# Quarter-wise stores, early loads for the second batch, and two moved pieces of setup in a fused graph network kernel

## The chip, the cores and the metric

The kernel runs on one core of one Trainium2 chip. The metric is the device time of the whole program in microseconds. A core has TensorE (PE) for matrix products, VectorE (DVE), ScalarE (ACT) and GpSimd (POOL) for the rest, and SyncE (SP), which here only issues transfers. POOL issues transfers too. The engines run side by side, each in its own program order, and wait for one another through semaphores.

## The reference

The input `x` has 128 samples of 128 nodes with 256 channels, `adj` is 128 x 128 for each sample, everything in float32. Two layers, each with a normalization in front and a residual:

```python
h = jnp.maximum(_layernorm(x, axis=-1), 0.0)
x = x + _L0_gnn_ref(h, adj, ...)
h = jnp.maximum(_layernorm(x, axis=-1), 0.0)
x = x + _L1_gnn_ref(h, adj, W1, b1, W2, b2, fusion_w)
```

Layer 0 computes from `h` a pointwise convolution, a convolution with 17 taps along the nodes with a residual, and a message passing term (a three-channel embedding, `exp` of minus squared distances, a product with `relu(x w_msg + b)`); both go into the gates of a GRU, 256 wide. Layer 1 takes five groups of the first 25 nodes (53 rows together), runs two graph convolutions on each (256 to 512 to 256), and adds the results, weighted with a softmax of the five `fusion_w`. So layer 1 changes only rows 0 to 24 of a sample; the other rows of the result are layer 0's.

## The kernel before

**Tiling.** Four samples make one `q`; there are 32 of them. The 17-tap convolution is done in a transformed domain of 80 points along the nodes, in two batches of 16 q each. Layer 1 works on blocks of four q (16 samples), eight blocks.

**Stages.** For each batch there is a *begin* and then *products*. The begin (`stage_a`, one call for each q) loads x of the q (`load_x`, L360, four transfers of 128 KB on SP's queue), takes mean and variance with `bn_stats` and `bn_aggr` on DVE and a `pow` on POOL (`moments`, L267 to L270), normalizes on DVE (L275), transposes on PE (`ph`, L387), stores the result to memory as `hTd` through POOL (L392), multiplies with the first convolution's weights (`pc`, L398) and transforms (`pf`, L409) into the large tile X. The products (`stage_b`) run over 40 frequencies f: load weights `wf` on SP (L488, three frequencies ahead), add on POOL (`add`, for f + 1), multiply on PE (`pa`, `pb`, L502), combine on DVE into `y` (L525), and store `yd` through POOL. Beside the first begin runs `tap_weights`, which transforms the convolution's weights (`pw`, L451) and stores them as `wfd`; beside everything after it runs `early(q)`, the message passing of each q (`pse`, `pm`, `pd`, `px`). Then a last, long stage runs the inverse transform and the gates for each q (`stage_c`), with what is left of `early`, and layer 1 (`rows`, `prepare`, `block`) beside it.

**What sets the order.** The order of the instructions is written by the program itself, when it is built. Every helper is a generator that yields two numbers: the time it believes its PE work takes, and the time until it can go on. `Lane` holds a row of such generators, of which `ahead` run at once; `Order.run` always takes the lane that has done least for its weight, and in it the one that is due. The second begin runs three lanes: `begin` with three q at a time, `beside` with weight 0.2, and `gates` (`fold_gates`, which loads and combines the gates' weights) with weight 0.5. What is late in a yield only fixes the place of an instruction in its engine's queue; on the chip the engine waits for what the instruction needs.

**Names that matter here.** In `stage_a`, a q loads itself and its successor, and if its own x was not there before, it yields 6 us (or 14 for the later ones of the second batch) before its statistics. `load_late` (L252, L253) loads `wse` (67 KB) and the second part of the constants `cst` (461.5 KB) on SP; it is called from `tap_weights` at step (n, m) = (2, 4) of 4 x 8. Nothing needs them before the end of that stage, in `fold_embedding`. The pool `tw`, closed when `tap_weights` ends, holds `wse`, two `wt`, one `wide` and three `ws` tiles of 16 KB per partition, and the pools `wg`, `io` and `fr` are opened in the same memory right after; a tile there waits until what lay in its place has been read or stored. `wmsg` and `bmsg` (L474, L475) are the first loads into `fr`, and the first loads of `hT` (L540) into `io` follow them on SP.

**The end.** `block` runs the two graph convolutions of a block and then, for each of its four quarters (one q each): `turn` (transposes on PE, L1062, a copy on ACT), `gather` (PE, L1074; then an addition on DVE, L1076, and a relu on ACT, L1077), `fuse` (PE with the fusion weights `s2w`, L1083; then an addition into x1 on DVE, L1085). Then four transfers on POOL's queue (L1094) store x1 of all four quarters. `setup_1` prepares layer 1; it loads `fus` and makes the softmax of the fusion weights on DVE and ACT (L895 to L906) into `s2w`.

Of the kernel before, what the change touches and what calls it, by code (L numbers as in the profile page):

```python
# [19 lines left out]
P = 128  # L20
# [187 lines left out]
def kernel(ctx: ExitStack, tc: tile.TileContext, x, adj, consts, vecs, w_se, conv1_w,  # L208
# [24 lines left out]
    def c(name):  # L233
        a, b = CAT[name]
        return cst[:, a:b]
# [13 lines left out]

    def load_late():  # L250

        nc.sync.dma_start(out=wse, in_=w_se.rearrange("(k p) o -> p k o", p=P))  # L252
        nc.sync.dma_start(out=cst[:, CFIRST:], in_=consts[:, CFIRST:])  # L253

    scl, sft = {}, {}
    brz = cp.tile([P, 4], FP, name="brz")
    wse9 = wp.tile([P, 2, WIDE], FP, name="wse9")
# [70 lines left out]
    def fold_embedding():  # L328
# [9 lines left out]
                                       op0=ALU.mult, op1=ALU.add)  # L338
        yield 1.5, 0.0

    lab, turn = ExitStack(), []
# [24 lines left out]
    def stage_a(q):  # L368
        ab = LATE["ab"]
        for n in range(q, min(q + 2, (q // BQ + 1) * BQ)):  # L370
            if n not in XA:
                load_xa(n)
                if n == q:
                    yield 0.0, 14.0 if q > BQ else 6.0
        if q not in MOM:
            MOM[q] = moments(XA[q], "a")
            yield 0.0, 3.0
            normalize(XA[q], XA[q], *MOM[q])
            yield 0.0, 2.0
        while q - 2 >= q // BQ * BQ and q - 2 not in A_DONE:  # L380
            yield 0.0, 0.5
        xn = XA[q]
        hT = ab.tile([P, 2, 512], FP, tag="hTa", name=f"hTa{q}")
        for cc in range(2):
            ph = ptmp.tile([P, 4, GB, WIDE], FP, tag="tmp", name=f"ph{q}_{cc}")
            for t in range(4):
                nc.tensor.transpose(ph[:, t].rearrange("p j n -> p (j n)"),  # L387
                                    xn[:, t, cc * P:(cc + 1) * P], ident)
            nc.scalar.activation(
                hT[:, cc].rearrange("p (j t n) -> p t j n", j=GB, t=4), ph, AF.Relu)  # L390
        yield 0.9, 2.4
        nc.gpsimd.dma_start(out=hTd[q], in_=hT)  # L392
        h1 = ab.tile([P, GB, D], FP, tag="h1", name=f"h1{q}")
        for h in range(2):
            pc = ptmp.tile([P, 2, D], FP, tag="tmp", name=f"pc{q}_{h}")
            for i in range(2):
                for k in range(2):
                    nc.tensor.matmul(pc[:, i], hT[:, k, (2 * h + i) * N:(2 * h + i + 1) * N],  # L398
                                     c1w[:, k], start=(k == 0), stop=(k == 1))
            s = slice(2 * h, 2 * h + 2)  # L400
            nc.vector.tensor_tensor(h1[:, s], pc, brow[:, None, :].to_broadcast([P, 2, D]),
                                    ALU.add)
            nc.scalar.activation(h1[:, s], h1[:, s], AF.Relu)
            yield 1.75, 2.8 * h
        for h in range(2):
            for k in range(2):
                pf = ptmp.tile([P, 2, D], FP, tag="tmp", name=f"pf{q}_{k}_{h}")
                for i in range(2):
                    nc.tensor.matmul(pf[:, i, :F * NB], h1[:, 2 * h + i, k * P:(k + 1) * P],  # L409
                                     fwd, start=True, stop=True)  # L410
                g0 = (q % BQ * GB + 2 * h) * NB
                dst = X[:, k, :, g0:g0 + 2 * NB].rearrange("p f (g b) -> p f g b", b=NB)
                src = pf[:, :, :F * NB].rearrange("p g (f b) -> p f g b", b=NB)
                if (k, h) == (0, 0):
                    nc.vector.tensor_copy(dst, src)  # L415
                else:
                    nc.scalar.activation(dst, src, AF.Copy)
            yield 1.1, 0.0
        A_DONE.add(q)
# [16 lines left out]
    def tap_weights():  # L436

        yield 0.0, 16.0
        for n in range(4):
            for m in range(8):  # L440
                if m == (0 if n else 3) and n < 3:
                    load_taps(n + 1, nc.sync, nc.gpsimd)
                if (n, m) == (2, 4):
                    load_late()
                if m % 2 == 0:
                    ws = tw.tile([P, 4, 4, D], FP, tag="ws", name=f"ws{n}_{m}", bufs=3)
                pws = [(pgat if r < 3 else ptmp).tile([P, 2, D], FP, tag="gat" if r < 3 else "tmp",
                                                      name=f"pw{n}_{m}_{r}") for r in range(4)]
                for r in range(4):
                    rows = slice(32 * r, 32 * r + TAPS)  # L450
                    nc.tensor.matmul(pws[r][:F], c("tap")[rows], wts[n][rows, 2 * m:2 * m + 2],  # L451
                                     start=True, stop=True)
                i = m % 2 * 2
                for r in range(4):
                    if r < 2 or (r == 2 and m % 2):
                        nc.scalar.activation(ws[:F, r, i:i + 2], pws[r][:F], AF.Copy)
                    else:
                        nc.vector.tensor_copy(ws[:F, r, i:i + 2], pws[r][:F])
                yield 0.9, 2.2
                if m % 2:  # L460
                    for r in range(4):
                        i0 = 64 * r + 16 * n + 2 * (m - 1)
                        nc.gpsimd.dma_start(out=wfd[:, i0:i0 + 4], in_=ws[:F, r])
# [4 lines left out]
        LATE["wn"] = wg.tile([P, 7, 2, P], FP, name="wn")  # L468
        LATE["wh"] = wg.tile([P, 7, 1, P], FP, name="wh")
        LATE["io"] = near.enter_context(tc.tile_pool(name="io", bufs=2, reuse_waits="tile"))  # L470
        LATE["fr"] = near.enter_context(tc.tile_pool(name="fr", bufs=1, reuse_waits="tile"))
        LATE["wmsg"] = LATE["fr"].tile([P, 2, D], FP, name="wmsg")
        LATE["bmsg"] = LATE["fr"].tile([P, D], FP, name="bmsg")
# [4 lines left out]
    def stage_b(bat):  # L478
# [29 lines left out]
        for f in range(NF + 1):  # L508
            if f + 3 <= NF:
                load_w(f + 3)  # L510
            if f < NF:
                add(f + 1)
            y = xf.tile([P, 2, D], FP, tag="y", name=f"y{bat}_{f}")
            pa = pgat.tile([P, 2, D], FP, tag="gat", name=f"pa{bat}_{f}")
            for s in range(2):
# [355 lines left out]
    def setup_1():  # L871
# [6 lines left out]
            tc.tile_pool(name="l2", bufs=2, reuse_waits="tile"))  # L878
        b2s = pool.tile([NG, D], FP, tag="dd", name="b2s")
        nc.sync.dma_start(out=b2s, in_=b2)  # L880
        fus = pool.tile([P, NG], FP, name="fus")
        nc.sync.dma_start(out=fus, in_=fusion_w.partition_broadcast(P))
        for n in range(2):
            load_w1(n)
        S["w2"] = weight(pool, W2, [P, 5, 4, D], "g (k p) o -> p g k o", "w2", nc.sync)
# [4 lines left out]
        for t in (*r4, S["yz"][:, 0], S["yz"][:, 1], S["b1"]):  # L890
            nc.gpsimd.memset(t, 0.0)
            yield 0.0, 4.0

        fmx = pool.tile([P, 1], FP, name="fmx")
        nc.vector.reduce_max(fmx, fus, axis=mybir.AxisListType.X)  # L895
        nc.vector.tensor_scalar(fus, fus, fmx, None, op0=ALU.subtract)  # L896
        nc.scalar.activation(fus, fus, AF.Exp)
        fsm = pool.tile([P, 1], FP, name="fsm")
        nc.vector.reduce_sum(fsm, fus, axis=mybir.AxisListType.X)
        nc.vector.reciprocal(fsm, fsm)  # L900
        nc.vector.tensor_scalar(fus, fus, fsm, None, op0=ALU.mult)
        nc.vector.tensor_mul(fus, fus, c("grp"))
        wrow = pool.tile([P, 1], FP, name="wrow")
        nc.vector.reduce_sum(wrow, fus, axis=mybir.AxisListType.X)
        s2w = S["s2w"] = pool.tile([P, 2 * WIDE], FP, name="s2w")
        nc.vector.tensor_scalar(s2w, c("s2"), wrow, None, op0=ALU.mult)  # L906
        b2row = S["b2row"] = pool.tile([P, D], FP, name="b2row")
        pb2 = ptmp.tile([P, 512], FP, tag="tmp", name="pb2")
        nc.tensor.matmul(pb2[:, :D], c("grpt")[:NG], b2s, start=True, stop=True)
# [92 lines left out]
    def block(blk):  # L1002
        while not (blk in P_DONE and blk - 1 in B1_DONE):
            yield 0.0, 0.5
        pool, yz, b2row, s2w = S["pool"], S["yz"], S["b2row"], S["s2w"]
        w2, ac, r4 = S["w2"], S["ac"][blk % 2], S["r4"][blk % 2]

        for q in range(QS):
# [48 lines left out]
        def turn(q):  # L1057
            pz = ptmp.tile([P, 2, D], FP, tag="tmp", name=f"pzt{blk}_{q}")
            for a in range(2):
                for cc in range(2):  # L1060
# [1 line left out]
                    nc.tensor.transpose(  # L1062
                        pz[:, a, cc * P:(cc + 1) * P],
                        yz[:, cc, b0:b0 + 2, :].rearrange("p s r -> p (s r)"), ident)
            zt = zts[q] = pool.tile([P, 2, D], FP, tag="zt", name=f"zt{blk}_{q}", bufs=3)
            nc.scalar.activation(zt, pz, AF.Copy)

        def gather(q):
# [10 lines left out]
        def fuse(q):  # L1079
            zt = zts.pop(q)  # L1080
            pf = ptmp.tile([P, D], FP, tag="tmp", name=f"pfu{blk}_{q}")
            for a in range(2):
                nc.tensor.matmul(pf[a * 2 * WIDE:(a + 1) * 2 * WIDE], s2w, zt[:, a],  # L1083
                                 start=True, stop=True)
            nc.vector.tensor_add(x1[:, q], x1[:, q], pf)  # L1085

        for what, q in ((turn, 0), (turn, 1), (turn, 2), (gather, 0), (gather, 1), (fuse, 0),
                        (turn, 3), (gather, 2), (fuse, 1), (gather, 3), (fuse, 2), (fuse, 3)):
            what(q)
            if (what, q) == (gather, QS - 1):  # L1090
                B1_DONE.add(blk)
            yield {turn: 0.45, gather: 0.9, fuse: 0.5}[what], 0.5
        for j in range(GB):
            nc.gpsimd.dma_start(  # L1094
                out=out[blk * SB:(blk + 1) * SB, :WIDE].rearrange("(q j) n c -> j n q c", j=GB)[j],
                in_=x1[j * WIDE:(j + 1) * WIDE])
        F_DONE.add(blk)


# [5 lines left out]
    load_xa(2)  # L1105
    fold()
    beside = Lane([tap_weights()] + [early(q) for q in range(NQ)])
    gates = Lane([fold_gates()], weight=0.5)
    for bat, (during_a, during_b) in enumerate(((0.66, 0.5), (0.2, 0.65))):
        if bat:  # L1110
            take_turn("ab", 2, reuse_waits="tile")
# [58 lines left out]
```

## Time and profile before

| | us |
|---|---|
| median of three runs | 2099.61 |
| lowest and highest of the three | 2089.95, 2099.69 |
| the profiled execution: device time | 2107.02 |
| its span, first to last instruction | 2105.2 |
| last matmul ends | 2098.1 |
| mean granted clock of TensorE in it | 0.986 |

The table by stage and the waits that matter are shown in the prediction. In such a table each row is a stretch of the span; for every engine it gives the time it was busy and, in brackets, how many instructions it ran. The granted clock is the share of full speed at which TensorE was allowed to run. In a list of waits each row reads: engine, tile, line, then what it waited for, the total in us, how often, and the longest. In a line of the timeline the first number is the start, the second the time, and the text in square brackets says how long the engine was idle before and what released it. "SPq" is SyncE's queue, where "x4" are four transfers issued in a row, and the second number is the time from the first to the end of the last issue.

The first 222 us are the first begin, 222 to 371 the first products, 371 to 540 the second begin, 540 to about 708 the second products; then comes the long last stage. From 2062 us on, only block 7 of layer 1 is left.

### The profile page before, as it was taken

What the parts mean: (1) busy time and instruction counts of PE and PEld (TensorE: products, weight loads), DVE (VectorE), ACT (ScalarE), POOL (GpSimd) and SP (SyncE); (2) the same over time, 40 slices, a digit from 0 to 9 for tenths busy, and PEclk for the clock granted to TensorE, in tenths of its full rate; (3) what the DMA queues carried; (4) which work ended last, traced back from release to release, by engine and by line L of the source; (5) the groups of instructions that cost most, each with busy time, mean ns of one, the idle gap of its engine ahead of it and who ended that gap; (6) DMA issues with size and microseconds to landing.
All of it is one profiled execution on the core that took longest, in us unless ns stands there. A gap on an engine that the chain in (4) does not pass through costs nothing.

```text
span 2105.2 us, 31050 instructions
## 1 busy us (share of the span) xinstructions
PE 2045.2 (97%) x11316; PEld 1657.3 (79%) x11316; DVE 1181.8 (56%) x2775; ACT 686.8 (33%) x1543; POOL 725.5 (34%) x902
## 2 busy tenths in 40 slices
PE   7978999999999999999999999999999999999998
PEld 5656888789888788787878877878787787878875
DVE  6754544786544455655654565565565655654642
ACT  4643222344222333323232232232233223223333
POOL 3432666232565222503322233224323323233230
PEclk9989999999999999999999999999999999999999
DMA  9977778744777634222323332323232333223121
GB/s 217 276 227 231 240 266 264 211 153 143 250 258 257 210 111 141 75 78 73 89 71 92 87 83 72 88 71 91 75 96 73 79 91 93 78 81 98 31 79 51
DMA packets 186870, 281.67 MB, mean 134 GB/s; under 512 B 20745, under 2 KB 139982, under 8 KB 186718
## 3 DMA queue, kind: packets, MB, share of 16 engines
q1 hardware_dynamic: 156270, 185.00, 31.0%
q0 software_dynamic: 30160, 94.46, 14.1%
q8 instruction: 90, 1.47, 0.3%
q14 instruction: 62, 0.51, 0.1%
q10 hardware_dynamic: 288, 0.22, 0.0%
HBM read 187.34 MB, written 92.27 MB: 133 GB/s over the span
## 4 chain that ended last, share of the span: by engine, by line
PE 91%; DMA 4%; DVE 2%; issue 1%; POOL 1%; ACT 0%; SPq 0%; POOLq 0%; DVEq 0%; ACTq 0%
PE p L709 41%; PE pa L502 7%; PE pm L601 5%; PE ph L1031 5%; PE pz L1040 5%; PE pc L398 4%; PE pb L502 3%; PE pi L674 3%; PE px L627 3%; PE pf L409 2%; PE pg L1074 1%; PE ph L387 1%; PE pc L688 1%; PE po L855 1%; DMA xa<-in_x 1%; PE py L1014 1%
## 5 line engine op out<-in xcount | busy, mean ns | idle before, releaser
L835 POOL TENSOR_TENSOR d<-hTc,r 128x512 f32<-128x512 f32 x64 | 81.3, 1271 | 370.9 <-ACT r L832 370.9
L502 PE MATMUL pa<-wf,X 128*128 128x256 f32 x640 | 152.5, 381 | 0.0
L864 POOL DMA_DIRECT2D out<-xt x128 | 71.9, 567 | 211.0 <-DVE xt L861 205.4
L525 DVE SCALAR_TENSOR_TENSOR y<-pa,kk 128x512 f32<-128x512 f32 x78 | 53.8, 690 | 147.0 <-ACT kk L524 147.0
L398 PE MATMUL pc<-c1w,hTa 128*128 128x256 f32 x512 | 125.4, 392 | 6.6 <-DVE X L415 4.3
L709 PE MATMUL p<-th,wrz 128*128 128x256 f32 x512 | 131.7, 380 | 0.0
L724 ACT ACTIVATE z<-z,brz 128x256 f32<-128x256 f32 x128 | 58.1, 501 | 225.5 <-DVE z L781 191.2
L709 PE MATMUL p<-tc,wrz 128*128 128x256 f32 x512 | 131.6, 380 | 0.0
L709 PE MATMUL p<-tm,wrz 128*128 128x256 f32 x512 | 131.5, 380 | 0.0
L502 PEld LDWEIGHTS pa<-wf,X 128*128 128x128 f32 x640 | 118.3, 190 | 16.2 <-issue 2.2
L601 PE MATMUL pm<-wmsg,hT 128*128 128x256 f32 x512 | 124.4, 389 | 0.0
L691 DVE SCALAR_TENSOR_TENSOR xc<-pc,s_bn,hTc 128x256 f32<-128x256 f32 x128 | 53.1, 478 | 118.3 <-PE pc L688 118.3
L398 PEld LDWEIGHTS pc<-c1w,hTa 128*128 128x128 f32 x512 | 96.0, 195 | 25.9 <-DVE X L415 4.5
L601 PEld LDWEIGHTS pm<-wmsg,hT 128*128 128x128 f32 x512 | 97.9, 194 | 16.7 <-issue 1.8
L1031 PE MATMUL ph<-yz,w 128*128 128x96 f32 (+3 forms) x640 | 109.2, 325 | 0.9 <-DVE yz L1016 0.9
L1033 ACT ACTIVATE hh<-ph,vec 128x96 f32<-128x96 f32 (+3 forms) x160 | 64.0, 402 | 134.2 <-PE ph L1031 124.7
L709 PEld LDWEIGHTS p<-tm,wrz 128*128 128x128 f32 x512 | 97.5, 190 | 13.0
L1040 PE MATMUL pz<-hh,w 128*128 128x96 f32 (+3 forms) x640 | 107.3, 322 | 0.0
L1031 PEld LDWEIGHTS ph<-yz,w 128*128 128x128 f32 x640 | 88.1, 193 | 21.9 <-issue 13.2
L709 PEld LDWEIGHTS p<-tc,wrz 128*128 128x128 f32 x512 | 95.2, 190 | 12.0 <-issue 0.5
L709 PEld LDWEIGHTS p<-th,wrz 128*128 128x128 f32 x512 | 94.9, 190 | 12.1 <-DVE fus L896 0.3
L709 PE MATMUL p<-hTc,wrz 128*128 128x256 f32 x384 | 103.9, 394 | 0.0
(204 smaller groups left out, 4562.0 us busy)
## 6 DMA issues: line engine op xcount, KB each, us to landing
wf<-wfd SPq DMA_DIRECT2D x160, 256.0 KB, 4.1
wfd<-ws POOLq DMA_DIRECT2D x64, 320.0 KB, 8.2
yd<-y POOLq DMA_DIRECT2D x80, 256.0 KB, 3.8
yt<-yd SPq DMA_DIRECT2D x64, 320.0 KB, 4.9
w<-in_W SPq DMA_DIRECT2D x40, 512.0 KB, 3.7
xa<-in_x SPq DMA_DIRECT2D x128, 128.0 KB, 5.2
hTd<-hTa POOLq DMA_DIRECT2D x32, 512.0 KB, 5.8
hT<-hTd SPq DMA_DIRECT2D x32, 512.0 KB
```

The costliest lines, as they stand in the source:

```text
L398: nc.tensor.matmul(pc[:, i], hT[:, k, (2 * h + i) * N:(2 * h + i + 1) * N], c1w[:, k], start=(k == 0), stop=(k == 1))
L502: nc.tensor.matmul(ps, xk(k), WF[f][:, k, s], start=(k == 0), stop=(k == 1))
L601: nc.tensor.matmul(pm[:, i], hT[:, k, j * N:(j + 1) * N], LATE["wmsg"][:, k], start=(k == 0), stop=(k == 1))
L627: nc.tensor.matmul(px[:, dc, i], msgs[h][:, i, dc * P:(dc + 1) * P], aT[:, 2 * h + i], start=True, stop=True)
L674: nc.tensor.matmul(pi[b * 64:(b + 1) * 64], inv[:F], yt[:, b::2], start=True, stop=True)
L709: nc.tensor.matmul(ps[:, m], w[:, i, k, m * P:(m + 1) * P], factor(i, x, t), start=first and j == 0, stop=last and j == len(n) - 1, skip_g ...
L724: nc.scalar.activation(dst[:, m], src[:, m], AF.Sigmoid, bias=brz[:, b + m:b + m + 1])
L835: nc.gpsimd.tensor_sub(d, hT[:, dc], r[:, dc])
L864: nc.gpsimd.dma_start(out=out[q * GB + j, WIDE:].rearrange("(t n) c -> n t c", n=WIDE), in_=xt[j * WIDE:(j + 1) * WIDE, 1:4])
L1031: nc.tensor.matmul(ph, w1[:, k, m * P:(m + 1) * P], yz[:, k, :, o:o + n], start=(k == 0), stop=(k == 1))
L1033: nc.scalar.activation(hh[:, m], ph, AF.Relu, bias=v("b1", g * 4 + m))
L1040: nc.tensor.matmul(pz, w2[:, g, m, cc * P:(cc + 1) * P], hs[g][:, m], start=(m == 0), stop=(m == 3))
```

## The change

There are five edits.

1. In the first batch's products, at f = 33, 36 and 39, x of q 16, 17 and 18 is loaded into three tiles of a new pool `xe` (4 KB per partition each). At f = 36 the statistics of q 16 are taken, at f = 38 it is normalized. In the second begin, q 17 then yields 1 us and q 18 12 us before their statistics.
2. `load_late` is called at step (1, 3) in place of (2, 4), and it also loads `fus`, the five fusion weights for all 128 partitions.
3. The softmax of the fusion weights leaves `setup_1` and becomes a generator `fold_fusion` behind `fold_gates` in the lane `gates`. `fus` and `s2w` become tiles of the constant pool.
4. x1 is stored after each quarter's `fuse`: in blocks 0 to 6 with one POOL transfer for each quarter, in block 7 with four transfers for each quarter, on SP, of which two of the last quarter go through ACT's queue.
5. The order of `turn`, `gather` and `fuse` in the four quarters changes, with a fourth `zt` buffer.

```diff
     def load_late():
+        nc.sync.dma_start(out=fus, in_=fusion_w.partition_broadcast(P))
         nc.sync.dma_start(out=wse, in_=w_se.rearrange("(k p) o -> p k o", p=P))
         nc.sync.dma_start(out=cst[:, CFIRST:], in_=consts[:, CFIRST:])
+    fus = cp.tile([P, NG], FP, name="fus")
+    s2w = cp.tile([P, 2 * WIDE], FP, name="s2w")
...
+    def fold_fusion():
+        fmx = cp.tile([P, 1], FP, name="fmx")
+        nc.vector.reduce_max(fmx, fus, axis=mybir.AxisListType.X)
+        nc.vector.tensor_scalar(fus, fus, fmx, None, op0=ALU.subtract)
+        nc.scalar.activation(fus, fus, AF.Exp)
+        yield 0.0, 4.0
+        fsm = cp.tile([P, 1], FP, name="fsm")
+        nc.vector.reduce_sum(fsm, fus, axis=mybir.AxisListType.X)
+        nc.vector.reciprocal(fsm, fsm)
+        nc.vector.tensor_scalar(fus, fus, fsm, None, op0=ALU.mult)
+        yield 0.0, 4.0
+        nc.vector.tensor_mul(fus, fus, c("grp"))
+        wrow = cp.tile([P, 1], FP, name="wrow")
+        nc.vector.reduce_sum(wrow, fus, axis=mybir.AxisListType.X)
+        nc.vector.tensor_scalar(s2w, c("s2"), wrow, None, op0=ALU.mult)
+        yield 0.0, 0.0
...
         if q not in MOM:
+            if BQ < q < BQ + 3:
+                yield 0.0, 11.0 * (q - BQ) - 10.0
             MOM[q] = moments(XA[q], "a")
...
-                if (n, m) == (2, 4):
+                if (n, m) == (1, 3):
                     load_late()
...
         LATE["io"] = near.enter_context(tc.tile_pool(name="io", bufs=2, reuse_waits="tile"))
+        LATE["xe"] = near.enter_context(tc.tile_pool(name="xe", bufs=1, reuse_waits="tile"))
         LATE["fr"] = near.enter_context(tc.tile_pool(name="fr", bufs=1, reuse_waits="tile"))
...
             if f < NF:
                 add(f + 1)
+            if f >= NF - 6 and f % 3 == 0 and bat + 1 < NBAT:
+                n = (bat + 1) * BQ + (f - NF + 6) // 3
+                XA[n] = LATE["xe"].tile([P, 4, D], FP, name=f"xa{n}")
+                load_x(XA[n], n)
+            n = (bat + 1) * BQ
+            if f == NF - 3 and n in XA:
+                MOM[n] = moments(XA[n], "a")
+            if f == NF - 1 and n in XA:
+                normalize(XA[n], XA[n], *MOM[n])
...
             nc.vector.tensor_add(x1[:, q], x1[:, q], pf)
+            b0 = blk * SB + q * GB
+            if blk < NBLK - 1:
+                nc.gpsimd.dma_start(out=out[b0:b0 + GB, :WIDE], in_=x1[:, q])
+                return
+            for j in range(GB):
+                eng = nc.scalar if q == QS - 1 and j % 2 else nc.sync
+                eng.dma_start(out=out[b0 + j, :WIDE], in_=x1[j * WIDE:(j + 1) * WIDE, q])
-        for what, q in ((turn, 0), (turn, 1), (turn, 2), (gather, 0), (gather, 1), (fuse, 0),
-                        (turn, 3), (gather, 2), (fuse, 1), (gather, 3), (fuse, 2), (fuse, 3)):
+        for what, q in ((turn, 0), (turn, 1), (turn, 2), (gather, 0), (turn, 3), (gather, 1),
+                        (gather, 2), (fuse, 0), (gather, 3), (fuse, 1), (fuse, 2), (fuse, 3)):
...
-        for j in range(GB):
-            nc.gpsimd.dma_start(
-                out=out[blk * SB:(blk + 1) * SB, :WIDE].rearrange("(q j) n c -> j n q c", j=GB)[j],
-                in_=x1[j * WIDE:(j + 1) * WIDE])
...
-    gates = Lane([fold_gates()], weight=0.5)
+    gates = Lane([fold_gates(), fold_fusion()], weight=0.5)
```

What `setup_1` loses is the same text as `fold_fusion`'s, without its yields, and the load of `fus`.

## The prediction

> **What bounds the kernel now.** I read the busy times first, then one row for each stage, then what TensorE (PE) waited for in the two stages where it idles, then the queue of SyncE (SP) in the first of them, and last the tail.
>
> ```profile
> PE 2045.2 (97%) x11316; PEld 1657.3 (79%) x11316; DVE 1181.8 (56%) x2775; ACT 686.8 (33%) x1543; POOL 725.5 (34%) x902
> ```
>
> PE is busy for 2045.2 of 2105.2 us, so 60 us of idle time, and the time at half clock, are all that this change can win: it removes no matmul. The stages (window, PE, weight loads, DVE, ACT, POOL, granted clock, DMA share, GB/s):
>
> ```profile
> 0.00:222.00 222.00, 188.51 (x1134) 136.09 (x1134) 135.19 (x362) 102.25 (x219) 80.16 (x120) 0.93 0.87 233
> 222.00:371.00 149.00, 149.00 (x896) 128.91 (x884) 69.97 (x119) 36.46 (x96) 94.95 (x118) 1.00 0.80 264
> 371.00:540.00 169.00, 160.76 (x1060) 141.50 (x1061) 122.09 (x332) 73.50 (x167) 47.61 (x58) 0.98 0.55 174
> 540.00:700.00 160.00, 160.00 (x987) 137.43 (x987) 72.20 (x137) 40.48 (x109) 98.37 (x123) 1.00 0.76 255
> 700.00:745.00 45.00, 40.59 (x245) 33.38 (x244) 24.09 (x57) 14.46 (x34) 2.15 (x4) 1.00 0.57 164
> 745.00:2062.00 1317.00, 1312.22 (x6791) 1054.81 (x6789) 750.51 (x1753) 406.70 (x890) 399.06 (x476) 0.99 0.30 84
> 2062.00:2105.00 43.00, 34.16 (x224) 25.20 (x224) 7.70 (x19) 12.97 (x29) 3.20 (x6) 0.93 0.21 61
> ```
>
> The first begin loses 33 us, both product stages nothing, the second begin 8, the long last stage about 5 in 1317, the tail 9. Who ended PE's waits, in the first begin and then in the second:
>
> ```profile
> PE pse L581 <- DMA hT<-hTd: 9.1, 1, 9.1
> PE pw L451 <- DVE X L415: 6.7, 1, 6.7
> PE pc L398 <- DVE X L415: 4.3, 1, 4.3
> ```
>
> ```profile
> PE pc L398 <- ACT ef L589: 2.3, 1, 2.3
> PE pf L409 <- ACT ef L589: 1.8, 1, 1.8
> PE pd L614 <- DVE msg L604: 1.3, 1, 1.3
> PE px L627 <- DVE aT L619: 0.9, 1, 0.9
> PE ph L387 <- PE pm L601: 0.9, 1, 0.9
> ```
>
> SP's queue in the first begin, and the last steps of the tail:
>
> ```profile
> 94.43 9.94 SPq L360 DMA_DIRECT2D xa<-in_x  x4
> 104.42 1.04 SPq L252 DMA_DIRECT2D wse<-in_w_se  x1
> 105.50 0.67 SPq L253 DMA_DIRECT2D cst<-in_consts  x1
> 109.08 28.83 SPq L360 DMA_DIRECT2D xa<-in_x  x16
> ```
>
> ```profile
> 2097.48 0.65 PE L1083 MATMUL pfu<-zt,s2w 128*64 128x256 f32 x4 [0.94 <-ACT zt L1077]
> 2098.18 0.42 DVE L1085 TENSOR_TENSOR x<-x,pfu 128x256 f32<-128x256 f32 x1 [1.09 <-PE pfu L1083]
> 2098.90 2.17 POOL L1094 DMA_DIRECT2D out<-x  x4 [35.87 <-DVE x L1085]
> ```
>
> From 60 to 122 us the DMA engines are full; the two waits "DVE X" are really x loads that came late: DVE stood in `bn_stats` for xa11 until 115.5 and for xa12 until 134.6.
>
> **What the Trainium skill says.** "TensorE: Matmul & The Clock Gate", section "What's actually happening": the clock falls to half after an idle window of about 3.4 us. The trace agrees on the factor (eight `pc` matmuls take 3.78 us after the stall at 114, else 1.89) but a gap of 1.79 us at 877 was enough (clock 0.66 from 880 to 890), so stalls cost more than their length. "DMA: Bandwidth & Descriptors", section "Issuing engines are not separate DMA queues": issuing from several engines saves only the sequencer's time. No stage here shows SP and ACT storing together, so this is not tested by the trace of before. "ScalarE: Activation LUTs", section "What ACT_TABLE_LOAD costs": about 1283 ns a load; the trace has 1283 ns at L897, for the softmax's Exp.
>
> **Part 1, x and statistics of the second batch's begin.** Before, xa16 was in hand at 365.6, but its statistics ran at 377.9 and its transposes at 382.0, because `stage_a` yields 6 and 14 us after a load. PE's idle from 372 to 399 is 0.91 + 1.33 + 0.86 + 1.79 + 0.25 = 5.1 us. The half clock adds 1.7 us (0.83 over 380 to 390), 0.3 (0.97 over 390 to 400) and 1.4 (0.86 over 400 to 410), 3.4 in all. A later stall (431 and 442: 2.25 + 0.57 = 2.8 us) comes from the same late start. Together 11.3 us. After the change q 16 starts with its transposes at once, q 17 goes one microsecond later with x in hand, and q 18 after 12. Followed by hand through the three lanes, this gives PE about 12.4 us of work in the first 13.4. I leave 1.0 us there, and half of the later stall (1.4): **-9.0 us**, from -11 to -4. The lower gain holds if DVE is the bound (22.6 of 30 us busy from 370 to 400; 4.3 of them move out).
> What it costs in the products: twelve x issues (0.43 each) on SP, which carries two `wf` loads per 4 us and is mostly idle, while the same 1.5 MB were loaded near this place before. On DVE, four stats and aggregates and a scale, 2.4 us, and four normalizations, 1.4 us, in a stage where it is 47% busy. One `pow` of 1.03 us on POOL (64% busy), behind which the yd store and `add(38)` wait about 3.5 us. `add(38)` is needed some 5.9 us later, so this is covered. Behind the statistics on DVE stand `y` and the `ef`, `lr`, `msg` of `early`, on which PE waits in order. **+0.5 us**, from 0 to +4 (2 us and a half clock, if `pd` stands right behind).
>
> **Part 2, constants.** `wse`, `cst` (528 KB) and `fus` (128 pieces of 20 B) leave SP's queue at 104 us and enter it between xa8 and xa9, near 62 us. SP issues at a pace set by landings, so xa12 and xa13 come two places sooner, and at the 250 to 280 GB/s of this stage some 2 us of transfer goes from in front of xa12. The same 2 us now lie in front of xa9, xa10 and POOL's stores, in a stretch that is as full: hTa waited 0.5 us at 80.9, so there is no slack at all there. A full pipe pays once either way: **-0.5 us**, from -4 to +5.
>
> **Part 3, the pool `xe`.** It stands between `io` and `fr` and moves `fr` 12 KB up. By the tile sizes, wmsg and bmsg then lie on the `ws` buffer used last but one, and no longer on the last. Their issues, 180.34 to 181.35, no longer stand in front of the first hT load, which still waits for the last `wfd` stores (landed 180.2). The 9.1 us stall shrinks by **-1.0 us** (0 to -1.2).
>
> **Part 4, softmax.** Seven small DVE operations, an Exp and its table load leave 850 to 853.6, where PE had no gap; in the second batch's gates lane they meet Exp already loaded: 0. A later `prepare` stall (1.79 us, then 6.8 us at half clock, 5.2 in all, at 877) may move with the order of instructions: from -5 to +5, **0** taken.
>
> **Part 5, stores and the order of the last quarters.** With `turn 3` earlier and `fuse 1` behind `gather 3`, the waits of 0.66 and 0.94 us go; the last gather starts at about 2093.6 in place of 2094.87, so the last x1 is ready at 2097.3, not 2098.6. But now 14 stores go through SP at 0.49 us each (180.34 to 182.79, five steps). The first can leave at 2094.3, so the last leaves at 2094.3 + 13 x 0.49 = 2100.7, where POOL's last left at 2100.5. What is late next is SP's own queue: **-0.5 us**, from -3 to +1. In blocks 0 to 6 POOL waits at four places in place of one; behind it stand the gate's `d` and the `pow` of `rows`, which PE reaches later, and POOL is 30% busy: 0.
>
> **Sum**: -9.0 + 0.5 - 0.5 - 1.0 + 0 - 0.5 = -10.5 us. The profiled execution took 2107.0 (span 2105.2 and 1.8 around it) and would come to 2096.5. The median shown is 2099.61, 7.4 lower, so 2089 us. One of the three runs was 2089.95, so the measurement itself moves by as much.
>
> **Rivals.**
> 1. Half of it. The wait at the second begin is DVE's order, not x: xa16 lay ready for 12 us, and DVE was 75% busy. Then part 1 gives -4, the sum is -5.5, and the time is 2094. For it: the `msg` and `ef` entries among the waits. Against it: the same DVE load from 440 to 480 (30.6 of 40 us) leaves PE 0.57 us of idle.
> 2. More. The constants help xa11 and xa12 fully (-4) and the stall at 877 goes (-5.2): 2080. For it: SP's queue above. Against it: the order is redrawn in eight blocks, and a new stall is as likely.
> 3. Slower, by the constants. `wse`, in 256 rows of 268 B, was in flight from 104.4 to 122.5. Put in front of xa9, it makes x late three times more before 114: the point is xa9 landing after 88.3, where its statistics start. Each such stall costs what the one at 114 did, 4.29 + 1.89 + 0.44 = 6.6 us; three give +19.8 against -10, 2109. Against it: SP is silent from 70.6 to 89.7, room to catch up.
>
> **How the numbers follow.** Forecast 0.42, rival 1 0.27, rival 2 0.15, rival 3 0.16. A change under 0.5% (10.5 us) cannot be told from none. The forecast sits on that bound: 0.22 faster, 0.20 same. Rival 1 gives 0.02 and 0.25, rival 2 all of its 0.15 to faster, rival 3 0.06 to same and 0.10 to slower. Faster 0.39, same 0.51, slower 0.10. The forecast's own range is 2083 to 2095; 2079 to 2103 takes in most of the others.
>
> **What would show it.** Right: `ph` of q 16 straight after the last product, no half clock from 381 to 402, the second begin 9 us shorter; hT's wait near 8; SP's stores back to back to the end. Wrong: PE gaps before 114, a gap in the products near f = 36, or a last stage that moves by more than 5 us.

## The result and the profile after

| | before | changed |
|---|---|---|
| median (11 runs each), us | 2095.65 | 2082.85 |
| lowest and highest, us | 2089.79, 2099.69 | 2077.34, 2086.57 |
| profiled execution, device time, us | 2107.02 | 2083.1 |
| its span, us | 2105.2 | 2081.3 |
| mean granted clock | 0.986 | 0.992 |

The ratio is 0.9946 with a 95% interval from 0.9929 to 0.9964, which is 11.3 us (7.5 to 14.9) faster. The two profiled executions differ by 24 us, twice as much; the first experiment below shows where.

The busy times of the changed kernel:

```profile
PE 2035.6 (98%) x11316; PEld 1651.2 (79%) x11316; DVE 1177.8 (57%) x2775; ACT 694.4 (33%) x1547; POOL 728.6 (35%) x898
```

The same matmuls, 9.6 us fewer of PE's time (before the last matmul 27 us are at half clock, before the change 55), and 45.7 us of idle time in place of 60. The table by stage, cut where the first and last product of each batch stands: first begin, first products, second begin, second products, a gap before the first gates, last stage, tail behind the last matmul (columns as in the prediction):

```profile
0.00:196.00 196.00, 172.54 (x1059) 123.51 (x1060) 128.75 (x351) 99.31 (x211) 74.85 (x116) 0.98 0.92 256
196.00:354.00 158.00, 158.00 (x951) 136.72 (x950) 78.89 (x142) 38.83 (x104) 100.11 (x124) 1.00 0.81 264
354.00:507.50 153.50, 146.50 (x961) 130.32 (x960) 110.77 (x308) 69.25 (x155) 47.67 (x56) 0.99 0.54 171
507.50:673.70 166.20, 166.20 (x1020) 142.59 (x1019) 70.73 (x142) 42.49 (x115) 97.21 (x122) 1.00 0.76 251
673.70:690.30 16.60, 14.82 (x122) 11.98 (x120) 11.73 (x27) 5.13 (x13) 1.62 (x3) 1.00 0.92 297
690.30:2075.10 1384.80, 1377.52 (x7215) 1106.02 (x7214) 776.51 (x1805) 439.43 (x952) 407.16 (x479) 0.99 0.30 84
2075.10:2081.30 6.20, 0.00 (x0) 0.00 (x0) 0.42 (x1) 0.00 (x0) 0.00 (x0) 0.66 0.27 64
```

Cut in the same places, the kernel before has 211.3, 157.9, 170.8, 166.7, 15.1, 1376.4 and 7.0 us. The second begin is 17 us shorter, but it also holds 16.1 us less of PE's work (146.5 busy us, before 162.6): the planner now lays less of `early` beside it (87 `pm` matmuls, before 119), and that work lies in the last stage, which is 8 us longer and has 8.2 us more of PE's work. So the second begin has to be read together with what follows: from its start to the last matmul the kernel before takes 1728.9 us, the changed one 1721.3.

What PE waited for in the first begin, and then in the second:

```profile
PE pse L614 <- DMA hT<-hTd: 7.1, 1, 7.1
PE pc L421 <- DVE X L438: 2.8, 1, 2.8
```

```profile
PE pc L421 <- ACT hTa L412: 2.5, 1, 2.5
PE pd L647 <- DVE h L424: 1.2, 1, 1.2
PE pf L432 <- ACT ef L622: 0.9, 1, 0.9
PE ph L410 <- DVE aT L652: 0.9, 1, 0.9
```

`pse` waits 2 us less for its hT. The second begin is not free of waits at all: it idles 7.0 us, where before it was 8.2. SP's queue in the first begin, first before the change, where `wmsg` stands right in front of hT, then changed, with the constants in their new place and `wmsg` well ahead of hT:

```profile
180.34 0.39 SPq L474 DMA_DIRECT2D wmsg<-in_w_msg  x1
...
181.35 0.37 SPq L540 DMA_DIRECT2D hT<-hTd  x1
```

```profile
59.87 2.50 SPq L381 DMA_DIRECT2D xa<-in_x  x4
62.41 0.43 SPq L252 DMA_DIRECT2D fus<-in_fusion_w  x1
63.66 0.38 SPq L253 DMA_DIRECT2D wse<-in_w_se  x1
65.08 0.34 SPq L254 DMA_DIRECT2D cst<-in_consts  x1
66.92 8.47 SPq L381 DMA_DIRECT2D xa<-in_x  x8
...
160.92 0.38 SPq L498 DMA_DIRECT2D wmsg<-in_w_msg  x1
161.35 1.87 SPq L499 DMA_DIRECT2D bmsg<-in_b_msg  x1
167.14 0.34 SPq L573 DMA_DIRECT2D hT<-hTd  x1
```

And the last steps of the tail:

```profile
2072.48 6.61 SPq L1109 DMA_DIRECT2D out<-x  x14
...
2074.44 0.65 PE L1100 MATMUL pfu<-zt,s2w 128*64 128x256 f32 x4 [0.51 <-ACT zt L1094]
2075.14 0.42 DVE L1102 TENSOR_TENSOR x<-x,pfu 128x256 f32<-128x256 f32 x1 [0.74 <-PE pfu L1100]
2075.59 0.83 ACTq L1109 DMA_DIRECT2D out<-x  x2
```

The last x1 is ready at 2075.56, and SP is still issuing until 2079.1: its queue is the late thing.

### The profile page after: what moved, and what is told of

The parts are those of the page before. It is cut to its first block, busy times and chain, and to the rows that moved or that the text cites. A ratio compares the mean times of both kernels' runs of the same rounds, so it can differ in the third digit from the quotient of the medians.

```text
span 2081.3 us, 31079 instructions
## 1 busy us (share of the span) xinstructions
PE 2035.6 (98%) x11316; PEld 1651.2 (79%) x11316; DVE 1177.8 (57%) x2775; ACT 694.4 (33%) x1547; POOL 728.6 (35%) x898
## 4 chain that ended last, share of the span: by engine, by line
PE 91%; DVE 4%; DMA 3%; ACT 1%; POOL 1%; issue 1%; SPq 0%; DVEq 0%; ACTq 0%; POOLq 0%
PE p L742 42%; PE pa L526 6%; PE pm L634 5%; PE ph L1048 5%; PE pz L1057 5%; PE pc L421 4%; PE pb L526 3%; PE pi L707 3%; PE pf L432 3%; PE px L660 2%; PE pg L1091 2%; PE po L888 1%; PE pc L721 1%; PE py L1031 1%; PE pw L474 1%; PE ph L410 1%
```

## The experiments

Differences in us are the ratio times the time before in the same series (2094.25, 2092.72, 2093.84 and 2093.3).

| run | ratio to before, 95% | us |
|---|---|---|
| e1 before, once more | 0.9998 [0.9985, 1.0010] | -0.4 |
| e2 before + constants early | 1.0002 [0.9990, 1.0015] | +0.4 |
| e3 changed, constants back | 0.9956 [0.9937, 0.9976] | -9.2 |
| e4 before + early x and pool | 0.9966 [0.9954, 0.9979] | -7.1 |
| e5 changed, early x and pool out | 0.9985 [0.9974, 0.9997] | -3.1 |
| e6 before + stores and order of the end | 0.9989 [0.9973, 1.0004] | -2.3 |
| e7 before + pool alone | 0.9993 [0.9982, 1.0004] | -1.5 |
| e8 changed, merged stores | 0.9939 [0.9918, 0.9960] | -12.8 |
| e9 changed, stores shared out | 0.9931 [0.9904, 0.9958] | -14.4 |
| e10 changed, gate sums later | 0.9938 [0.9914, 0.9962] | -13.0 |
| e11 before, gate sums later | 0.9978 [0.9967, 0.9990] | -4.6 |
| e12 changed, e9's stores and gate sums later still | 0.9913 [0.9887, 0.9938] | -18.2 |

### The first begin and the constants (e1, e2, e3)

e1 is the kernel before without an edit. e2 moves `load_late` alone, and e3 takes that move out of the changed kernel:

```diff
-                if (n, m) == (2, 4):
+                if (n, m) == (1, 3):
                     load_late()
```

> The kernel before once more, for a second profile of it. Theory A (the two stalls of the first begin, 4.3 us at 114 and 6.7 us at 131, are fixed by the order of SyncE's queue): they return within 1 us, and the first product starts at about 211 us as before. Theory B (they are an accident of one execution: the transfers of this stage interleave differently each time): the stage is some 5 to 10 us shorter or the stalls lie elsewhere, and part of the profiles' 15 us in this stage is not the change's. Time ratio to before 1.00 in both.

> Only the call of load_late moves, from step (2, 4) to (1, 3). Theory A (the constants stood in front of xa12 and xa13, and the moved load takes the stall at 131 with its half clock): -8 to -14 us, ratio 0.993 to 0.996, with one stall left near 114. Theory P (as predicted, a full pipe pays once either way): -4 to +3 us, ratio 0.998 to 1.0015.

> The changed kernel with load_late back at step (2, 4). Theory A: the gain of the change is nearly gone, -2 to -5 us against before (0.9975 to 0.999), the stall near 131 is back, and the first product starts at about 208 to 211 us. Theory P: the gain stays, -9 to -12 us (0.994 to 0.996).

The profiled execution of e1 spans 2096.2 us, 9 less than the first one of the same program, and the difference lies in the first begin: 200.6 us, before 211.3. The wait of 6.7 us at 131 is not there, the one at 114 takes 3.8 us. So up to 10.7 of the 15.4 us that this stage lost between the two profiles of the result can belong to the execution and not to the change. e2 and e3 agree with each other and with an effect of nothing: the interval of e2 reaches from -2.1 to +3.1 us, and that of e3 covers the changed kernel's ratio. In the profile of e2 the first begin has the stalls of e1, 4.2 us at 117 and 9.4 at 173, and at 81 it has one of 0.9 us, where before had 0.5.

### Early x, and the pool that came with it (e4, e5, e7)

e4 adds to the kernel before the loads, statistics and normalization in the products, the yields and the pool `xe`. e5 takes exactly these out of the changed kernel. e7 adds the pool alone: three tiles of it receive two numbers each from POOL and are never read, and nothing is loaded early.

```diff
+        LATE["xe"] = near.enter_context(tc.tile_pool(name="xe", bufs=1, reuse_waits="tile"))
         LATE["fr"] = near.enter_context(tc.tile_pool(name="fr", bufs=1, reuse_waits="tile"))
...
+            if f >= NF - 6 and f % 3 == 0 and bat + 1 < NBAT:
+                xe = LATE["xe"].tile([P, 4, D], FP, name=f"xe{f}")
+                nc.gpsimd.memset(xe[:, 0, :2], 0.0)
```

> The kernel before with the x loads, statistics and normalization of the second batch's begin in the products, the pool xe and the two yields, nothing else. Theory P (prediction): second begin 9 us shorter in net terms, in all -8 to -10 us with the 1 us of wmsg, ratio 0.995 to 0.9965. Theory A (from the profile of the change: idle and half clock of the second begin fell from 8.2 + 3.4 to 7.0 + 1.7): -2 to -5 us, ratio 0.9975 to 0.999.

> The changed kernel without the x loads, statistics and normalizations in the products, without the two yields and without the pool xe; fusion softmax, constants, quarter-wise stores and the new order of the last quarters stay. Theory P (part 1 with its pool is worth about 9.5 us, as predicted): the rest brings 2 to 3 us, ratio to before 0.9985 to 0.9992, no less. Theory Q (the prefetch is worth about half, and the rest of the gain comes from the tail and from the order of the last stage): ratio 0.9960 to 0.9980, and the last stage or the tail is shorter by 3 us or more.

> The kernel before with the pool xe between io and fr, and in it three tiles that receive two numbers each from POOL and are never read: so fr lies 12 KB higher, and nothing is prefetched. Theory P: wmsg and bmsg no longer stand in front of the first hT load, which comes 1 to 2.5 us sooner: the wait of the first pse goes from 9.1 to about 7, and the time falls by 1 to 2.5 us, ratio 0.9988 to 0.9995. Theory R: the wait only moves to the next loads in SP's queue, the first begin keeps its length, and the ratio is 1.000. Theory S: the pool itself brings most of what the kernel with the prefetch alone gained, ratio 0.997.

e4 brings 7.1 us (4.4 to 9.6), less than expected of the theory of the prediction and more than of its rival. e5, everything but these edits, brings 3.1 (0.6 to 5.4), at the upper edge of what theory P expected. The two add up to 10.2, and the whole change has 11.3. In e7's list of waits:

```profile
PE pse L585 <- DMA hT<-hTd: 7.1, 1, 7.1
```

In the eight kernels with the pool this wait is 6.0 to 7.9 us; in the six without it, 8.7 to 9.5. So the pool shortens it by some 2 us with no x in it. The 1.5 us by which e7 is faster fit that, but their interval (-3.8 to +0.8) includes zero. In the profiles the whole first begin is shorter with the pool, 193.1 to 199.1 us against 198.9 to 211.3. That gap overstates it: the profiled executions of the six without the pool happen to lie 0.2 to 11.4 us above their kernels' medians, those of the eight between 4.7 below and 1.6 above. Early x itself is then worth about 7.1 - 1.5 = 5.6 us alone, and 11.3 - 3.1 - 1.5 = 6.7 us beside the other edits; each is a difference of numbers that are uncertain by 2 to 4 us. In no profile did the first products change: 157.9 us in each kernel.

### The end (e6, e8, e9)

e6 is the kernel before with the quarter-wise stores, the new order of the quarters and the fourth `zt` buffer. In e8 the first three quarters of block 7 are stored in one transfer each. e9 merges nothing, but gives the third quarter to ACT:

```diff
+            if q < QS - 1:
+                nc.sync.dma_start(out=out[b0:b0 + GB, :WIDE], in_=x1[:, q])
+                return
             for j in range(GB):
```

```diff
-                eng = nc.scalar if q == QS - 1 and j % 2 else nc.sync
+                eng = nc.scalar if q == QS - 2 or q == QS - 1 and j % 2 else nc.sync
```

> The kernel before with part 5 alone: quarter-wise stores, four zt buffers and the new order of turn, gather and fuse. Theory P: -0.5 us (from -3 to +1), ratio 0.9985 to 1.0005, because SP's 14 issues become the late thing in the tail, and POOL's four waits per block cost nothing. Theory Q: the order of quarters also takes small waits away in all eight blocks, so -4 us, ratio 0.998, and the last stage is shorter by 3 us or more.

> The changed kernel, with one store in place of four for each of the first three quarters of the last block (the last quarter keeps two stores on SP and two on ACT). SP then issues 5 stores in place of 14. Theory P (SP's queue is the late thing of the tail): SP is free when the last x1 is ready, its last issue ends about 1 us after that and not 3.5 us after it, and the tail behind the last matmul falls from 6.2 to about 4 us: 2 to 2.5 us faster than the changed kernel, ratio to before near 0.9935. Theory T (the landing of the stores, not their issue, sets the end): the tail stays at 6 us and the ratio at 0.9946.

> The changed kernel, with the third quarter's four stores of the last block issued by ACT and no longer by SP: each of SP and ACT issues eight of 32 KB, none is merged. Merging three quarters into stores of 128 KB took the issues off SP, and the tail only fell from 6.2 to 5.9 us, since each merged store landed 3 us or more after its issue. Theory P (SP's queue is late, and 32 KB stores land in about 1.5 us): the last issue ends near 1.5 us after the last x1 instead of 3.5 us, the tail behind the last matmul falls from 6.2 to about 4.7 us, ratio to before 0.9935 to 0.9940. Theory T (whatever issues them, 16 stores so close together land no sooner): tail 5.9 to 6.2 us and ratio 0.9946.

How long a store takes from issue to landing, first in the kernel before, then in the changed one (median, last number):

```profile
out<-x POOLq DMA_DIRECT2D x32, 128.0 KB, 2.8
```

```profile
out<-x POOLq DMA_DIRECT2D x28, 128.0 KB, 4.3
out<-x SPq DMA_DIRECT2D x14, 32.0 KB, 1.5
out<-x ACTq DMA_DIRECT2D x2, 32.0 KB, 1.6
```

Put on a line from the last matmul's end, by the trace's issues and completion events: before, the last issue starts 2.4 us later, lands 2.9 after that, and the program ends 1.9 after the landing, in which POOL still drains; together 7.1. Changed: 3.6, 1.6 and 1.1, together 6.2. SP's queue is later by 1.2 us, and that is paid back by a landing 1.3 us quicker and an end 0.8 us quicker.

The last matmul itself also comes sooner, so this line doesn't hold the whole gain. The products `pz` of block 7 stand ahead of the four quarters and end at 2087.80 and 2066.07:

```profile
2084.08 3.72 PE L1040 MATMUL pz<-hh,w 128*128 128x96 f32 x32
```

```profile
2062.35 3.72 PE L1057 MATMUL pz<-hh,w 128*128 128x96 f32 x32
```

From there to the last x1 it is 10.80 us before and 9.49 changed, to the start of the last issue 12.72 and 12.60, and to the end of the program 17.45 and 15.26. The new order brings the last x1 1.3 us sooner, SP's queue uses that up, and the quicker landing and end bring 2.2 us. In e5 and e6 the end comes at 15.04 and 15.05, so 2.4 us sooner, which is about what e6 gains in the timed runs (2.3, from -0.8 to 5.7).

e8 refuted the guess that the queue alone matters. Its last issue starts 1.0 us after the last matmul (3.6 in the changed kernel), and the tail is still 5.9 us. The three merged stores landed 3.4 to 4.3 us after their issue. That of the third quarter was issued at 2068.41 and completed at 2072.67, its data through four completion events, after an early one at 2069.38; each of the 32 KB stores of the changed kernel has sixteen. The Trainium skill, "DMA: Bandwidth & Descriptors", section "Why a DMA increments its semaphore by 16 and not by 1", says that a transfer uses the largest number of engines, at most 16, that divides the slowest dimension of both sides: four here (four samples), sixteen in the unmerged stores (32 rows); what is missing to sixteen the issuing sequencer counts up at once. The four events and the early one agree. But the merged stores are not the last to land. The last quarter's four stores of 32 KB, issued from 2069.01 to 2069.54, landed at 2072.75 to 2073.28, 3.8 us after their issue on average, where in the changed kernel such stores take 1.5 or 1.6. In each of them four of the sixteen events come 0.4 us behind the other twelve, which fits merged stores ahead of them on four engines; why the twelve are late as well stays open. e9 keeps the small stores and shares them out:

```profile
2072.52 4.83 SPq L1109 DMA_DIRECT2D out<-x  x10
2074.46 2.82 ACTq L1109 DMA_DIRECT2D out<-x  x6
```

Both queues end at 2077.3, 1.7 us after the last x1, and the tail falls to 4.6 us. That theory P holds is shown by the trace; the timed ratio, 0.9931, lies on the right side of the changed kernel's 0.9946, but its interval includes that one.

### What is left in the second begin (e10, e11, e12)

The prediction put the stall that ends at 431 in the kernel before down to x that started late. The timeline of the kernel before around it:

```profile
423.90 1.83 POOL L323 TENSOR_TENSOR wrz<-wrz 128x768 f32<-128x768 f32 x1
424.29 5.12 DVE L275 TENSOR_SCALAR xa<-xa,mv,rs 128x256 f32<-128x256 f32 x4
426.79 1.82 POOL L323 TENSOR_TENSOR wrz<-wrz 128x768 f32<-128x768 f32 x1
429.34 0.40 DVE L586 TENSOR_SCALAR ef<-pse,cst,embb 128x128 f32<-128x128 f32 x1
...
431.21 1.13 PE L398 MATMUL pc<-c1w,hTa 128*128 128x256 f32 x4 [2.25 <-ACT ef L589]
```

Four normalizations took 5.12 us; at 406 in the changed kernel four take 1.37. Beside the four in 5.12 us POOL ran two additions of `fold_gates` (L323). In the changed kernel another instruction meets them:

```profile
402.43 2.60 DVE L625 TENSOR_TENSOR lr<-ef 128x256 f32<-128x256 f32 x1 [0.53 <-ACT ef L622]
402.92 1.82 POOL L326 TENSOR_TENSOR wrz<-wrz 128x768 f32<-128x768 f32 x1
404.96 1.28 DVE L424 TENSOR_TENSOR h<-pc,brow 128x512 f32<-128x512 f32 x2
405.73 0.63 ACT L426 ACTIVATE h<-h 128x512 f32<-128x512 f32 x1 [3.33 <-DVE h L424]
406.27 1.07 ACT L412 ACTIVATE hTa<-ph 128x512 f32<-128x512 f32 x2
...
406.90 1.59 PE L421 MATMUL pc<-c1w,hTa 128*128 128x256 f32 x5 [2.45 <-ACT hTa L412]
```

This is read from the bottom: PE waits 2.45 us for hTa on ACT, which stands behind `h` on ACT, which waits for `h` on DVE, which stands behind `lr`, and `lr` took 2.60 us. Of the 32 `lr` in this trace, the 17 that no POOL instruction overlaps took 0.42 to 0.43 us each, and the 14 that a POOL addition overlaps 0.47 to 3.14. The Trainium skill says in "SBUF — State Buffer", section "SBUF: two separate sides", that DVE and GpSimd share one pair of ports as an exclusive lock, for DVE's operations in a two-port mode or with two inputs from SBUF (the latter only against a GpSimd operation that reads SBUF, as these additions do), and that the first to start gets it. `lr` has two such inputs. `h`, which reads PSUM, keeps its 0.67 to 0.69 us in all 64 cases, with a POOL addition beside it or not. That the two engines hold each other up agrees with the trace; the order of starts doesn't show in it, since `lr` is recorded as starting 0.49 us before the addition. The normalizations have one tensor input, and whether they run in a two-port mode no run here shows. The experiments move POOL's 15 operations of `fold_gates` (twelve sums, three changes of sign) behind the begin: by 100 us in the changed kernel (e10) and in the kernel before (e11), and by 120 us in e12, which also has the stores of e9. In e10 and e12 the softmax, next in the same lane, moves with them.

```diff
+        yield 0.0, 100.0
         for w in (wrz, wn, wh):
             for dst, a, b, op in ((6, 0, 4, ALU.subtract), (4, 4, 3, ALU.add),
```

> The kernel before, with the same 15 additions of POOL 100 us later and nothing else. The prediction put the stalls of 2.25 and 0.57 us in the second begin down to x's late start. Theory D: they come from four normalizations that took 5.12 us beside two additions on wrz instead of 1.4 us, so they go, with their half clock, although x starts as late as before: 3 to 5 us, ratio 0.9975 to 0.9985. Theory X: they stay, ratio 1.000.

> The changed kernel, with POOL's 15 additions on wrz, wn and wh put 100 us later, so that they run beside the products of the second batch and not beside its begin. Theory D (what is left of the second begin's stalls is DVE stretched by POOL: lr took 2.60 us beside an addition on wrz, 0.42 otherwise, and PE then waited 2.45 us for hTa): that wait and its half clock go, second begin to the end of the last stage 3 to 5 us shorter, ratio to before 0.992 to 0.9935. Theory X (the stall is x or ACT coming late): the wait of 2.45 us stays or moves, ratio 0.9946.

> The changed kernel with both: the third quarter's stores on ACT, and POOL's 15 additions on wrz, wn and wh 120 us later (with 100 us the first two of them met another lr right at the start of the products, which then took 4.54 us and cost PE 2.88 us). Theory D: the waits of 2.45 and 0.88 us in the second begin go and no new one of more than 1.5 us stands at the start of the products; tail 4.6 us; together 4 to 6 us below the changed kernel, ratio to before 0.9915 to 0.993. Rival: lr is stretched by the additions on xs and wf in any case, a wait of 2 to 3 us stays at the start of the products, and only the tail's 1.6 us are left, ratio 0.993 to 0.994.

In e11 the stalls of 2.25 and 0.57 us are gone although x starts as late as before, and the time falls by 4.6 us (2.1 to 6.9). That is about as much as early x brings. The same four normalizations, in e11:

```profile
411.70 1.43 DVE L275 TENSOR_SCALAR xa<-xa,mv,rs 128x256 f32<-128x256 f32 x4
```

That another order of PE's work removed the stalls can be ruled out: in e11 PE's matmuls follow each other as in the kernel before until long after them (516 us there), and in e10 and e12 as in the changed kernel from the second begin to the end. In e10 the waits of 2.45 and 0.88 us in the begin go too, but the first two sums meet an `lr` right at its end:

```profile
501.06 1.27 POOL L522 TENSOR_TENSOR wf<-wf 128x512 f32<-128x512 f32 x1
501.73 4.54 DVE L626 TENSOR_TENSOR lr<-ef 128x256 f32<-128x256 f32 x1 [0.53 <-ACT ef L623]
502.29 1.80 POOL L327 TENSOR_TENSOR wrz<-wrz 128x768 f32<-128x768 f32 x1
...
506.32 0.97 PE L648 MATMUL pd<-lr 32*128 32x128 f32 x7 [2.88 <-DVE lr L626]
```

So most of the gain is given back at once: between the two ratios, e10's and the changed kernel's, lie 1.7 us, well within the intervals, and the ratio that theory D expected, 0.9935 at most, was missed. e12 moves them past that place. Its second begin, all that PE waited for:

```profile
PE pd L648 <- DVE h L425: 1.2, 1, 1.2
PE pf L433 <- ACT ef L623: 0.9, 1, 0.9
PE pd L648 <- ACT hTa L413: 0.6, 1, 0.6
PE pf L433 <- DVE aT L653: 0.5, 1, 0.5
```

3.2 us of idle time and no half clock, and no wait at the start of the products. With a ratio of 0.9913 it is the fastest of all kernels here, 18.2 us below the one before; its interval leaves out the changed kernel's 0.9946, but the two intervals overlap. Kernels whose PE runs the same matmuls in the same order from the second begin to the last matmul stand in one row, with the range of their profiles (e9, which differs from the changed kernel only in its stores, has a row for its tail):

| kernel | idle and half clock in the second begin, us | from its start to the last matmul, us | tail, us |
|---|---|---|---|
| before, e1, e2, e7 | 7.3 to 8.2 and 3.4 to 10.2 | 1727.2 to 1730.6 | 7.0 to 7.1 |
| e4 early x | 7.0 and 3.4 | 1724.9 | 7.1 |
| e5, e6 stores and order | 8.3 and 6.8; 7.6 and 3.4 | 1726.6; 1726.0 | 6.0; 6.0 |
| changed, e3, e8 | 7.0 and 0 to 3.4 | 1717.4 to 1721.3 | 6.2; 6.5; 5.9 |
| e9 | 7.0 and 3.4 | 1719.6 | 4.6 |
| e10 sums later | 6.1 and 0.2 (3.2 more right behind it) | 1718.2 | 6.3 |
| e11 before, sums later | 6.0 and 3.4 | 1723.1 | 7.0 |
| e12 | 3.2 and 0 | 1714.8 | 4.6 |

Executions of one order differ by up to 3.9 us on this way, so a smaller difference between two profiles shows nothing by itself. The clock is part of it: the changed kernel and e9 have 3.4 us at half clock after the wait of 2.45 us, e3 and e8 have the same wait and none. At half clock a matmul takes twice as long (eight `pc` 3.78 us in place of 1.89), so half of such time is lost.

## Why the prediction was right, and where its steps were not

The sum was -10.5 us and the measured difference is -11.3. The total is right, but terms of it are off in opposite directions, so that it comes this close is in part luck.

- **Part 1 (-9.0, and +0.5 in the products): right in direction, probably too large.** Measured about -5.6 to -6.7. With the pool it is 7.1 us (4.4 to 9.6) in e4, where the prediction's terms make 9.5, so the timed runs do not quite exclude it. The cost in the products was nothing that shows. Of the four or five waits between 372 and 399, 5.1 us, 3.2 are left, where "I leave 1.0 us there" stood. And the step "comes from the same late start" was wrong: that stall was DVE held up by POOL's sums. The sums stayed, so in the changed kernel it is no shorter (0.49 + 2.45 + 0.88 us, before 2.25 + 0.57), on another instruction. The rest of the gain came back in half clock (6.8 to 3.4 us in this pair) and in the gap after the second products (idle 4.1 to 1.8 us). Of the 4.3 us of DVE's work said to move out, the prediction's own terms, 2.4 and 1.4, make 3.8.
- **Part 2 (-0.5): right as far as can be told**, +0.4 (-2.1 to +3.1) in e2. "A full pipe pays once either way" is not contradicted; rival 3, three more late x, did not come.
- **Part 3 (-1.0): right mechanism, too small in the trace.** hT's wait fell by 2 us and not by 1; the timed runs give 1.5, with an interval that includes zero.
- **Part 4 (0): right.** No run has it alone, but e5 contains it beside the end and the constants, e6 only the end, and they differ by 0.8 us. The stall at 877 is unmoved by it: 1.80 us at 867 in e5 and at 870 in e6. With early x it becomes 2.48 us at 856. Exp was found loaded, as predicted: the softmax has no table load of its own at 491. Beside early x the move may be worth more than nothing: in e4, where the softmax stays at 846 to 850, PE waits 1.54, 1.89 and 1.86 us right behind it, in the changed kernel 0.73 and 2.48.
- **Part 5 (-0.5): order and queue were foreseen, what follows the last issue was left out.** The last x1 comes 1.3 us sooner, as the step has it, and SP's queue uses that up. By the step's own sum the last issue leaves at 2100.7 in place of 2100.5, so its -0.5 doesn't follow from that sum. From the start of the last issue to the end it is 2.7 us with SP's stores and 4.7 with POOL's, and so the end gains 2.2 to 2.4 us. The timed runs give 2.3 (-0.8 to 5.7) in e6 and 3.1 (0.6 to 5.4) in e5, which has parts 2 and 4 too.

Of the signs of being right, `ph` of q 16 stands at 355.4, one `pm` behind the last product, and SP's stores are back to back to the end. One sign of being wrong, a last stage that moves by more than 5 us, did appear: it is 8.4 us longer. The step had not reckoned with `early` moving there, but that is work in another place, not lost time: PE idles 7.3 us in it, before 7.0. ACT pays for the new mixture with more table loads, 12 of 1283 ns where the kernel before has 8 (e4 has 14).

Rival 1 (part 1 worth 4 us, because DVE's order is the limit) was nearer to the truth in its reason than the forecast: the wait was DVE's, but what stretched DVE was POOL.

## What to carry to other kernels

Before a stall is put down to a late input, compare the duration of the instruction that it waits behind with the same instruction elsewhere: four operations in 5.12 us instead of 1.37 pointed at a neighbour engine, not at x. In a tail, count from a product that both orders share to the end of the program, by issue, landing and drain, and share small stores over two queues; a merged store saves issues, but it can land later and so can the small ones behind it. And when a program plans its own order, read a shorter stage together with those that follow, because work leaves it as well as waits.

## What the runs showed of the hardware

- A DVE operation with both inputs in SBUF was stretched by POOL's additions: `lr` took 0.42 us alone, 2.60 beside one addition of 1.82, and 4.54 beside several in a row. `h`, which reads PSUM, took 0.67 to 0.69 us either way.
- Three stores of 128 KB with four samples as their slowest dimension landed in 3.4 to 4.3 us (e8), and the stores of 32 KB behind them in 3.8 on average; with no merged store ahead (changed kernel), stores of 32 KB, issued one after the other in 0.47 us each, landed in 1.5 or 1.6 us each.
- One and the same program had a first begin of 211.3 and of 200.6 us in two executions. In this stretch the DMA engines are 0.89 busy in the kernel before.
- Half clock came in pieces of 3.4 us or multiples of it. A gap of 1.79 us was followed by 6.8 us of it, one of 2.45 us by 3.4 us in two profiles and by none in two others.
